# Four graph layers on one core: the order of loads, norms and row preparation where one layer hands over to the next

## The chip, the cores and the metric

The kernel runs on one core of a Trainium2 chip. The metric is the device time of one execution in microseconds (us); lower is better. The core has a matrix engine (TensorE, PE in the profile), a vector engine (DVE), an activation engine (ACT), GpSimd (POOL) and SyncE (SP). Transfers are issued here by SP and by POOL, each into a queue of its own, and run on the same 16 DMA engines. Every engine works through its own instructions in order; an instruction whose input is not ready holds everything behind it on that engine.

## The reference, cut to what matters

A graph with 3327 nodes and 512 features a node passes through four layers. After each one the layer's input is added and every row is normalised.

```python
# layer 0: 8 heads of 64                       layer 2: 8 heads, elu;  layer 3: 4 heads of 128, elu
Wh = einsum('ni,hio->hno', x, W)               # projection
e  = leaky_relu(f1[:, :, None] + f2[:, None, :], 0.2)
att = softmax(where(adj > 0, e, -9e15))        # over the neighbours of a row
y  = einsum('hnm,hmo->hno', att, Wh)
x  = layernorm(x + y)                          # layers 2 and 3: layernorm(x + elu(y))

# layer 1: mean over the first 64 neighbours of a row
keep = (adj > 0) & (cumsum(adj > 0, axis=1) <= 64)
cnt  = keep.sum(axis=1)
xj = leaky_relu((keep @ x / max(cnt, 1)) @ W_nb.T + b_nb)
xi = leaky_relu(x @ W_line.T + b_line)
x  = layernorm(x + xi + where(cnt > 0, xj, 0))
```

## The kernel before, in words

The 3327 rows are padded to 26 tiles of 128 rows, t = 0 to 25; `NT` is 26 and `HALF` is 13. The layers follow one another on the matrix engine. The order of the matrix engine's instructions is written out by hand (`tc.manual_schedule`). The order on the other engines, transfers included, is made by a scheduler from the order in the source and its own estimates of cost; a single instruction can be held in its place in the source with `tc.keep_in_program_order(ins)`, called "pinned" below. Transfers of each issuing engine take eight completion counters in turn, so that a transfer waits at issue until the one eight places before it in the same queue has landed.

**What ends an attention layer.** The attention of layers 0 and 2 leaves sums for 26 tiles in memory (`hd`). The last section's output is copied out of PSUM (`ob`), transposed on the matrix engine (`pt`, L883), copied to `hb` (ACT, L890) and stored to `hd` by SP (L894). The next layer then reads rows back in pairs of tiles, `t0` = 0, 2, 4 and so on. `finish_steps` gives the steps for one pair: load `h` from `hd` and the layer's input as `xr`; divide by the softmax sum (`divide`, DVE, L186); in layers with elu take `e = exp(h)` (ACT, L193); add (DVE, L201 and L202 with elu, L204 without); then `norm_rows`. `norm_rows` takes the statistics of both tiles (DVE, L157 and L158), then one inverse root for the two tiles together (POOL, L148 and L149), the bias (DVE, L162), and scales each tile (ACT, L165).

**Layer 1, `sage`.** First part, per tile: the normed rows are transposed (PE, L1193, `pt`), copied to `xT` (ACT, L1195) and multiplied with the neighbour weights `wn` (PE, L1201, `pz`) and the line weights `wl` (PE, L1204, `pi`); the rows of the next pair are finished alongside. `wn`, `wl` (1 MB each) and the bias `blb` come through POOL's queue. So do the carries `cy` (L1131, 256 KB each), which start the running count of neighbours in a block of columns, and of which the first is used when tile 14 is reached (`carry_in(0)`). SP's queue brings the first mask block `mb` in 13 loads of 64 KB (L1148) and `cr`, one row of counts (L1215, 6.5 KB), which ACT turns to float as `cf` (L1225) for a transpose that stands at t0 = 8. The second part is the neighbour sum (L1303) with the rest of the layer.

**Layer 3, `third`.** For each tile: transposes (PE, L271), copy to `xT` (ACT, L272), a row sum (DVE, L273), and eight matmuls in two banks for the projection (PE, L281, `pw`), then small copies (ACT, L282 and L285) and scaled values (`vt`; DVE L291, ACT L289), which SP stores. The matrix engine is one tile ahead: it transposes tile t and then multiplies tile t - 1. `load_group(t0)` starts the steps of a later pair; its steps run in the source behind the transposes of the pair two earlier. `third` holds `load_group` and calls `finish_steps(..., pinned=t0 == 2)`.

When tile 14 (`HALF + 1`) has been transposed, the columns of the first half are complete, and `L3.prepare(pp, 0)` prepares the row factors: a clamp on DVE and an exponential on ACT over `rc` (`clamp`, L323 and L326), 13 small transposes on PE in quads of four (`quad`, L332, `pr`), a copy of each quad (ACT, L334, `rr`) and its store by SP, then the scales (`scales`, L338 to L346). Behind it stand the load of the first rows `rba` (`rows`, POOL) and `cut` (L369 on), all of them used where the attention of layer 3 begins (L416 and L478).

Of the kernel before, what the change touches and what calls it, by code (L numbers as in the profile page):

```python
# [32 lines left out]
def kernel(  # L33
# [114 lines left out]
        return [nc.gpsimd.tensor_scalar(out, var, LN_EPS, None, op0=ALU.add),  # L148
                nc.gpsimd.tensor_tensor(out, out, power[:, :n], op=ALU.pow)]  # L149

    def norm_rows(pool, ys, t0):
        n = len(ys)
        st = pool.tile([P, 4, 6], F32, name="st")
        mv = pool.tile([P, 4, 2], F32, name="mv")
        rs = pool.tile([P, 4, 2], F32, name="rs")
        for s, y in enumerate(ys):
            nc.vector.bn_stats(out=st[:, s, :], in_=y)  # L157
            nc.vector.bn_aggr(out=mv[:, s, :], in_=st[:, s, :])  # L158
        rsqrt(rs[:, :n, 0], mv[:, :n, 1])
        if t0 + n == NT:  # L160
            nc.vector.tensor_tensor(rs[:, n - 1, 0:1], rs[:, n - 1, 0:1], valid, op=ALU.mult)
        nc.vector.scalar_tensor_tensor(rs[:, :n, 1], mv[:, :n, 0], -1.0, rs[:, :n, 0],  # L162
                                       op0=ALU.mult, op1=ALU.mult)
        for s, y in enumerate(ys):
            nc.scalar.activation(y, y, AF.Identity, bias=rs[:, s, 1:2], scale=rs[:, s, 0:1])  # L165
# [3 lines left out]
    def finish_steps(pool, xin, layer, t0, n, hbufs=6, eng=nc.sync, xbufs=None, xpool=None, ebufs=None, pinned=False,  # L169
                     together=False):  # L170
        H, D = layer.H, layer.D
        ys, xs, steps = [], [], []

        def load():
            for t in range(t0, t0 + n):
                xr = xpool.tile([P, F], F32, name="xr", tag="hb") if xpool else \
                    pool.tile([P, F], F32, name="xr", bufs=xbufs)
                h = pool.tile([P, F], F32, name="h", bufs=hbufs)
                load_tile(h, hd, t, eng)
                ys.append(h)  # L180
                load_tile(xr, xin, t, nc.sync if layer.li == 2 else nc.gpsimd)
                xs.append(xr)

        def divide(s):
            h = ys[s]
            ins = nc.vector.tensor_tensor(h.rearrange("p (h d) -> p h d", h=H), h.rearrange("p (h d) -> p h d", h=H),  # L186
                                          rec[:, t0 + s, :H].rearrange("p (h e) -> p h e", e=1).to_broadcast([P, H, D]),
                                          op=ALU.mult)
            if pinned and t0 > 2:
                tc.keep_in_program_order(ins)  # L190
            if layer.elu:
                e = pool.tile([P, F], F32, name="e", bufs=ebufs)
                ins = nc.scalar.activation(e, h, AF.Exp)  # L193
                if pinned and layer.li == 2 and (t0, s) == (2, 0):
                    tc.keep_in_program_order(ins)
                xs.append(e)

        def add(s):
            h, xr = ys[s], xs[s]
            if layer.elu:  # L200
                nc.vector.scalar_tensor_tensor(xr, xs[n + s], 1.0, xr, op0=ALU.min, op1=ALU.add)  # L201
                nc.vector.scalar_tensor_tensor(h, h, 0.0, xr, op0=ALU.max, op1=ALU.add)  # L202
            else:
                nc.vector.tensor_tensor(h, h, xr, op=ALU.add)  # L204

        steps.append(load)
        if pinned or together:
            steps += [lambda s=s: divide(s) for s in range(n)] + [lambda s=s: add(s) for s in range(n)]
        else:
            for s in range(n):  # L210
                steps += [lambda s=s: divide(s), lambda s=s: add(s)]
        steps.append(lambda: norm_rows(pool, ys, t0))
        return ys, steps

    def finish(*a):
# [897 lines left out]
    def sage(first, first_pool, xin, prev, nxt, wsrc, dst, ring):  # L1113
# [5 lines left out]
        with tc.tile_pool(name="sg_z", bufs=1, reuse_waits="tile") as zp, \  # L1119
# [12 lines left out]
                                    .rearrange("(o t) i -> o t i", o=1).to_broadcast([P, n, GW]))  # L1132
                carry[b, t] = cy

            load_carry()
            load_carry()
            zs_ = [zp.tile([P, HALF, 2, F], F32R, name=f"zs{i}") for i in range(2)]

            def zs(t, c):
# [41 lines left out]
            with tc.tile_pool(name="sa_w", bufs=1, reuse_waits="tile") as wp, \  # L1181
# [37 lines left out]
                for t0 in range(0, NT, 2):  # L1219
                    ys = ahead  # L1220
                    if t0 in (6, 10):
                        prev.late.pop(0)(fp)
                    if t0 == 8:
                        cf = fp.tile([NT, P], F32, name="cf", bufs=1)
                        nc.scalar.copy(cf, cr)  # L1225
                        pt = ps.tile([P, FC, P], F32, name="pt")
                        cb = pt[:, 0, :NT]
                        nc.tensor.transpose(cb, cf, ident[:NT, :NT])
                        nc.vector.tensor_scalar(cnt[:, 0, :], cb, NEIGHBOURS, 1.0, op0=ALU.min, op1=ALU.max)
                        nc.vector.reciprocal(cnt[:, 1, :], cnt[:, 0, :])  # L1230
                        nc.vector.tensor_scalar(cnt[:, 2, :], cb, 0.0, None, op0=ALU.is_gt)
                    for s, y in enumerate(ys):
                        xT = step1(y)
                        if s == 0 and t0 + 2 < NT:
                            ahead = finish(fp, xin, prev, t0 + 2, 2, 6, nc.sync if t0 else nc.gpsimd, None, None, None,
                                           t0 < 6)
                        if pend:
                            step2(*pend)
                        pend = (y, xT, t0 + s)
                        if t0 == NT - 2 * FIRST // 2 - 4 and s == 1:  # L1240
                            seed(qp, "q")
                            carry_in(0)
                            carry_in(1)
                        if t0 + s >= NT - FIRST - 2 and len(kts) < 2 * FIRST:
                            kept()
                            k = len(kts) // 2
                            if k + 1 < FIRST:
                                carry_in(k + 1)
                    if t0 == 0:

                        step2(*pend)
                        pend = None
# [86 lines left out]
    def third(first):  # L1339
        with tc.tile_pool(name="col3", bufs=1) as cp:  # L1340
# [5 lines left out]
            with tc.tile_pool(name="p_w", bufs=1, reuse_waits="tile") as wp, \  # L1346
                    tc.tile_pool(name="p", bufs=3, reuse_waits="tile") as pp, \
                    tc.tile_pool(name="p_f", bufs=2, reuse_waits="tile") as fp, \
                    tc.tile_pool(name="p_ps", bufs=2, space=PSUM, reuse_waits="tile") as ps:
                wsb = wp.tile([P, FC, 2, FW + L3.H], F32, name="wsb")  # L1350

                def bank(e):
                    return ps.tile([P, 512], F32, name=f"pw{e}")


                pend = None
                ahead = first
                groups = []

                def load_group(t0):  # L1360
                    if t0 < NT:
                        groups.append(finish_steps(fp, x2, L2, t0, 2, 10, nc.gpsimd if t0 < 4 else nc.sync, 6,
                                                    pinned=t0 == 2))
                        groups[-1][1].pop(0)()

                load_group(2)
                load_wide(wsb, w3, nc.gpsimd)
                nc.vector.tensor_copy(wsb[:, :, :, FW:], wa[3].rearrange("p c (e h) -> p c e h", e=2))
                load_group(4)
                for t0 in range(0, NT, 2):  # L1370
                    ys = ahead
                    if t0 in (4, 8):
                        L2.late.pop(0)(fp)
                    load_group(t0 + 6)
                    for s, y in enumerate(ys):
                        t = t0 + s
                        store_tile(x3, y, t, nc.sync)
                        xT = L3.project1(pp, ps, y, t)
                        if s == 0 and groups:
                            ahead, steps = groups.pop(0)  # L1380
                            for f in steps:
                                f()
                        if pend:
                            L3.project2(pp, bank, wsb, *pend)
                        pend = (xT, t)
                        if t == HALF + 1:
                            L3.prepare(pp, 0)
                            L3.first_rows = L3.rows(rp, 0, 0)
                            L3.cut(pp, 0, "pc", 1, False, True)
                    if t0 == 0:  # L1390

                        L3.project2(pp, bank, wsb, *pend)
                        pend = None
                L3.project2(pp, bank, wsb, *pend)
                L3.mean(pp, bank, wsb)
# [332 lines left out]
```

## Time and profile before

| | us |
|---|---|
| median of three runs (lowest, highest) | 3219.51 (3215.29, 3220.92) |
| the profiled execution's own time | 3223.41 |
| its span in the trace | 3221.7 |
| PE busy | 3135.2 (97% of the span) |
| DVE, ACT, POOL busy | 2609.5, 2185.6, 322.5 |
| layer 1 begins (first `pz`) | 962.75 after the span's start |
| layer 3 begins (first `pw`) | 2417.45 after the span's start |

All durations in this document come from the profiled execution, whose mean granted clock of the matrix engine was 0.988; its time is 1.7 us more than its span. Line numbers with an L are those of the kernel before.

How the views are read. A **timeline** line gives the start, the busy time, the engine, the line, the operation, and in brackets the idle time of the engine just ahead of the line with what ended it. A line of **waits** says which engine and line waited for which other one, with the total, the number of times and the longest. The **DMA view** of a stretch gives packets and bytes for each queue: q0 is POOL's, q1 is SP's. **Windows** give the busy time of each engine in a stretch and, as PEclk, the share of the matrix engine's clock that was granted.

### The profile page before, as it was taken

To read this page: it belongs to the slowest core of one execution; us is meant where nothing else is said; L and a number is where in the kernel's file an instruction comes from. 1 tells how busy PE (TensorE), PEld (TensorE's weight loads), DVE (VectorE), ACT (ScalarE), POOL (GpSimd) and SP (SyncE) were. 2 spreads that over 40 slices of the span, in tenths; PEclk is the share of its full clock that TensorE was granted. 3 is DMA by queue.
4 is the path that set the end of the run, shared out by engine and by line. 5 is a ranking of instruction groups with operands and counts; after the bars stand their busy time and mean duration, and the time that the engine had idled before them with its cause. 6 is when DMAs were issued, how large, how long until landed. Compare 5 with 4: busy or idle time off the path is not lost. (4 is left out here: it accounts for less than half of the span.)

```text
span 3221.7 us, 44965 instructions
## 1 busy us (share of the span) xinstructions
PE 3135.2 (97%) x17910; PEld 1596.6 (50%) x17910; DVE 2609.5 (81%) x2228; ACT 2185.6 (68%) x1759; POOL 322.5 (10%) x512
## 2 busy tenths in 40 slices
PE   8899999999999999999999999999999999999997
PEld 7643343333334457777744333333337655555543
DVE  5799999999986555555489999999998666678887
ACT  1388889899882222232288889899896655568886
POOL 3110000000011112222220000000002000011211
PEclk9999999999999999999999999999999999999999
DMA  9752113211025345556341110111027311122312
GB/s 363 270 153 75 42 51 123 73 45 43 24 75 153 98 115 146 131 134 160 98 145 61 42 36 20 41 42 42 25 71 247 126 41 43 43 56 93 90 44 69
DMA packets 359985, 301.80 MB, mean 94 GB/s; under 512 B 232756, under 2 KB 291966, under 8 KB 358239
## 3 DMA queue, kind: packets, MB, share of 16 engines
q1 hardware_dynamic: 329471, 194.55, 20.7%
q0 software_dynamic: 24784, 96.68, 9.6%
q10 hardware_dynamic: 5520, 7.69, 0.7%
q8 instruction: 142, 2.33, 0.3%
q14 instruction: 68, 0.56, 0.1%
HBM read 221.97 MB, written 76.84 MB: 93 GB/s over the span
## 5 line engine op out<-in xcount | busy, mean ns | idle before, releaser
L842 ACT ACTIVATE y<-t,bi,sc 128x3328 fp8e4<-128x3328 f32 (+1 forms) x520 | 1336.2, 2604 | 99.4 <-PE pd L819 47.3
L863 PE MATMUL po<-t,vj 128*64 128x448 f32 (+1 forms) x6656 | 1277.4, 523 | 14.0 <-DVE t L841 13.9
L863 PEld LDWEIGHTS po<-t,vj 128*64 128x64 f32 x6656 | 459.3, 137 | 691.7 <-issue 622.7
L478 PE MATMUL po<-t,vj 128*128 128x448 f32 (+1 forms) x1456 | 522.6, 516 | 0.6 <-DVE t L416 0.6
L416 DVE SCALAR_TENSOR_TENSOR t<-rba,qc,mk 128x1664 f32<-128x1664 f32 (+2 forms) x234 | 408.4, 1752 | 125.8 <-PE po L478 88.5
L421 ACT ACTIVATE y<-t,bi,sc 128x1664 fp8e4<-128x1664 f32 (+2 forms) x234 | 375.3, 1618 | 190.1 <-DVE t L416 181.7
L478 PEld LDWEIGHTS po<-t,vj 128*128 128x128 f32 x1456 | 272.1, 190 | 235.2 <-issue 148.8
L841 DVE SCALAR_TENSOR_TENSOR t<-rbb,qc,mask 128x3328 f32<-128x3328 f32 (+1 forms) x130 | 379.9, 2982 | 10.0 <-PE po L863 6.5
L841 DVE SCALAR_TENSOR_TENSOR t<-rbb,qc,mk 128x3328 f32<-128x3328 f32 (+1 forms) x130 | 379.4, 2993 | 8.6 <-PE po L863 6.5
L841 DVE SCALAR_TENSOR_TENSOR t<-rba,qc,mk 128x3328 f32<-128x3328 f32 (+1 forms) x130 | 379.7, 2985 | 5.8 <-PE po L863 3.5
L841 DVE SCALAR_TENSOR_TENSOR t<-rba,qc,mask 128x3328 f32<-128x3328 f32 (+1 forms) x130 | 380.9, 2983 | 4.0 <-PE po L863 3.2
L1303 PE MATMUL acc<-zs,kt 128*128 128x512 f32 x1352 | 360.2, 420 | 0.0
L281 PE MATMUL pw<-wsb,xT 128*128 128x264 f32 (+1 forms) x1248 | 297.7, 393 | 11.8 <-DVE vt L291 8.1
L1161 ACT CAST pk<-cy 128x512 f32<-128x512 bf16 x169 | 99.6, 590 | 288.4 <-DVE kt L1175 281.9
L1303 PEld LDWEIGHTS acc<-zs,kt 128*128 128x128 f32 x1352 | 255.6, 189 | 52.1 <-PE pk L1154 0.8
L819 PE MATMUL pd<-y,sden 128*32 128x384 fp8e4 (+1 forms) x3328 | 270.2, 343 | 0.0
L281 PEld LDWEIGHTS pw<-wsb,xT 128*128 128x128 f32 x1248 | 238.4, 194 | 54.8 <-issue 6.5
L1175 DVE SCALAR_TENSOR_TENSOR kt<-pk,mb 128x512 fp32r<-128x512 f32 x169 | 115.9, 686 | 107.1 <-PE pk L1172 107.0
L819 PEld LDWEIGHTS <-sden 128*32 128x32 bf16 x3328 | 89.0, 95 | 166.7 <-issue 151.2
L291 DVE TENSOR_TENSOR vt<-pw,dc 128x256 f32<-128x256 f32 x130 | 49.8, 417 | 78.1 <-ACT dc L282 76.0
L1201 PE MATMUL pz<-wn,xT 128*128 128x512 f32 x208 | 94.0, 595 | 7.7 <-ACT xT L1195 3.7
L1131 POOL DMA_DIRECT2D cy<-ctd x91 | 70.1, 770 | 267.3 <-ACT pk L1161 243.4
(244 smaller groups left out, 2163.6 us busy)
## 6 DMA issues: line engine op xcount, KB each, us to landing
raw<-in_adjT_dram SPq DMA_DIRECT2D x67, 416.0 KB
vj<-v SPq DMA_DIRECT2D x169, 128.0 KB
cy<-ctd POOLq DMA_DIRECT2D x78, 256.0 KB, 4.3
h<-hd SPq DMA_DIRECT2D x61, 256.0 KB
v<-vt SPq DMA_DIRECT2D x50, 256.0 KB
md<-mask SPq DMA_DIRECT2D x26, 416.0 KB
mb<-md SPq DMA_DIRECT2D x169, 64.0 KB
mk<-md SPq DMA_DIRECT2D x50, 208.0 KB
```

Of the source, the lines that this page charges most:

```text
L281: nc.tensor.matmul(pw[e][:, :FW + H], xT[:, c, :], wsb[:, c, e, :], start=c == 0, stop=c == FC - 1)
L416: ins = nc.vector.scalar_tensor_tensor(t[:, :w], rb[:, lo:lo + w], self.qc[:, j, h:h + 1], mask_at[0](j, i0 + lo, w), op0=ALU.max, op1=ALU ...
L421: nc.scalar.activation(y[:, :w], t[:, :w], AF.Sigmoid, bias=self.bi[:, j, h:h + 1], scale=self.sc[:, j, h:h + 1], saturate=False)
L478: nc.tensor.matmul(po[c][k * D:(k + 1) * D, :z - a_], vj[:, j % 2, k * D:(k + 1) * D], ts[k][:, a_:z], start=j == 0, stop=j == NT - 1)
L819: nc.tensor.matmul(pd[c][32 * kk:32 * kk + 32, :w_], lhsT, rhs, start=(kk, c) not in seen, stop=last and j == NT - 1)
L841: nc.vector.scalar_tensor_tensor(to, ro, self.qc[:, j, h:h + 1], m, op0=ALU.max, op1=ALU.mult)
L842: nc.scalar.activation(yo, to, AF.Sigmoid, bias=self.bi[:, j, h:h + 1], scale=self.sc[:, j, h:h + 1], saturate=False)
L863: nc.tensor.matmul(po[c][k * D:(k + 1) * D, :z - a_], vj[:, j % 2, x_:x_ + D], t[:, k, a_:z], start=j == 0, stop=j == NT - 1)
L1161: nc.scalar.copy(pks[k % 2], carry[b, t // 4 * 4][:, t % 4:t % 4 + 2, :])
L1175: nc.vector.scalar_tensor_tensor(kt, pk, NEIGHBOURS, mb[:, t:t + 2, :], op0=ALU.is_le, op1=ALU.mult)
L1201: nc.tensor.matmul(pz, xT[:, c, :], wn[:, c, :], start=c == 0, stop=c == FC - 1)
L1303: nc.tensor.matmul(acc, kts[b, t][:, s * P:(s + 1) * P], zs(t, c), start=t == 0 and c == 0, stop=t == NT - 1 and c == 1)
```

## The change

Four things are done. The first two carries are loaded at t0 = 6 of `sage` instead of ahead of `wn` and `wl`. The first pair of tiles (t0 = 0) of layers 0 and 2 is normed one tile at a time, with an inverse root for each tile, and in layer 2 its statistics are pinned. In `divide`, the pin that was asked for with `pinned and t0 > 2` is asked for with `pinned or layer.li == 2 and t0 == 4`; `load_group` passes `pinned` for t0 = 2, so the divides of the pairs t0 = 2 and t0 = 4 of layer 2 are now held in the order of the source. In `third`, the clamp of `prepare` stays behind tile 14 and the rest of `prepare`, the load of the first rows and `cut` stand behind tile 15.

```diff
-    def norm_rows(pool, ys, t0):
+    def norm_rows(pool, ys, t0, pinned=False):
...
-            nc.vector.bn_aggr(out=mv[:, s, :], in_=st[:, s, :])
+            ins = nc.vector.bn_aggr(out=mv[:, s, :], in_=st[:, s, :])
+            if pinned:
+                tc.keep_in_program_order(ins)
...
-            if pinned and t0 > 2:
+            if pinned or layer.li == 2 and t0 == 4:
                 tc.keep_in_program_order(ins)
...
                 steps += [lambda s=s: divide(s), lambda s=s: add(s)]
-        steps.append(lambda: norm_rows(pool, ys, t0))
+                if t0 == 0 and layer.li != 3:
+                    steps.append(lambda s=s: norm_rows(pool, ys[s:s + 1], t0 + s, layer.li == 2))
+        if t0 or layer.li == 3:
+            steps.append(lambda: norm_rows(pool, ys, t0))
...
-            load_carry()
-            load_carry()
...
+                    if t0 == 6:
+                        load_carry()
+                        load_carry()
                     for s, y in enumerate(ys):
                         xT = step1(y)
...
                         if t == HALF + 1:
-                            L3.prepare(pp, 0)
+                            parts = L3.prepare_steps(pp, 0)
+                            parts.pop(0)()
+                        if t == HALF + 2:
+                            for f in parts:
+                                f()
                             L3.first_rows = L3.rows(rp, 0, 0)
                             L3.cut(pp, 0, "pc", 1, False, True)
```

On the matrix engine the order differs in one place only: the 13 transposes of L332 stand one tile later. What the built program does with the order on the other engines is told in the prediction.

## Prediction

> **What bounds the kernel now.** I read the page's first part, the waits around both passages, and there the timelines of each engine, the DMA view and the clock.
>
> ```profile
> PE 3135.2 (97%) x17910; PEld 1596.6 (50%) x17910; DVE 2609.5 (81%) x2228; ACT 2185.6 (68%) x1759; POOL 322.5 (10%) x512
> ```
>
> The matrix engine is busy for 97% of the span, so the change is worth what it takes from or adds to PE's few idle stretches. In the waits of 950 to 980 us, where layer 1 begins, these stand:
>
> ```profile
> PE pz L1201 <- ACT xT L1195: 2.9, 1, 2.9
> ...
> PE pz L1201 <- DMA wn<-in_wnT_dram: 2.7, 1, 2.7
> ACT cf L1225 <- DMA cr<-ctd: 2.6, 1, 2.6
> PE pt L883 <- ACT hb L890: 2.5, 1, 2.5
> ```
>
> PE loses 2.53 + 2.67 + 2.90 = 8.1 us here. The third line is ACT waiting for the row of counts; it harms nobody, as ACT makes `cf` after both `xT`. SP's timeline and the DMA view of 962 to 969 us show why that row is late:
>
> ```profile
> 958.98 7.59 SPq L894 DMA_DIRECT2D hd<-hb  x3
> 966.63 4.84 SPq L1148 DMA_DIRECT2D mb<-md  x6
> 971.79 0.33 SPq L1215 DMA_DIRECT2D cr<-ctd  x1
> ```
>
> ```profile
> q0 software_dynamic: 694, 2.43, 86.6%
> q1 hardware_dynamic: 675, 0.38, 17.5%
> ```
>
> While POOL's large loads drain, both queues advance about 97 packets/us (694/7 and 675/7), but POOL's packets are 4 KB and SP's 512 bytes or so. SP's first `hd` store (512 packets) takes 957.15 to 968.22. The layer 3 passage, on PE's timeline:
>
> ```profile
> 2410.53 0.33 PE L883 MATMUL pt<-ident,ob 128*128 128x128 f32 x1 [1.27 <-ACT hb L890]
> 2415.65 1.97 PE L271 MATMUL pt<-ident,h 128*128 128x128 f32 x8 [4.79 <-ACT h L165]
> 2417.45 9.35 PE L281 MATMUL pw<-wsb,xT 128*128 128x260 f32 x32
> ...
> 2433.56 0.66 PE L271 MATMUL pt<-ident,h 128*128 128x128 f32 x4 [1.13 <-ACT h L165]
> ```
>
> and its windows, where the column behind the five engines is the granted clock:
>
> ```profile
> 2409.00:2415.60 6.60, 0.60 (x4) 0.17 (x2) 4.54 (x11) 1.67 (x4) 0.96 (x2) 0.68 0.95 291
> 2415.60:2420.00 4.40, 4.35 (x14) 3.64 (x15) 4.37 (x9) 3.83 (x7) 0.00 (x0) 0.50 0.93 333
> 2420.00:2424.00 4.00, 4.00 (x15) 3.29 (x15) 3.41 (x8) 1.11 (x6) 2.73 (x2) 0.79 0.93 305
> ```
>
> The two first projections take 9.35 us where later ones take 3.67 each (2434.05): 2.0 us are lost to the clock after the wait. The row preparation costs two waits:
>
> ```profile
> 2481.89 1.04 PE L332 MATMUL pr<-ident,rc 128*4 128x128 f32 x8 [1.98 <-ACT rc L326]
> 2483.47 1.22 PE L332 MATMUL pr<-ident,rc 128*4 128x128 f32 x5 [0.55 <-ACT rr L334]
> ```
>
> **A. Layer 1's start.** The built order has `wn` where the first carry stood, so it is issued at about 953.3 instead of 955.64. The norm by tiles frees `hb` from both L165 (1.52 us): the 2.53 us wait goes. It adds a POOL pair (0.23 + 0.73) and a DVE L162 (0.16), beside idle stretches of both. The carries (two issues of 0.80) come on POOL after the next pair's loads, and stay due only at tile 14, past 1050 us; free.
>
> Two orders change besides. ACT now has `cf` ahead of both `xT`, and SP has five `mb`, three `hd`, eight `mb`, then `cr`. The last three `mb` wait for the three `hd` to land, and `cr` follows them. So a new wait stands on ACT, with `xT`(0), hence `pz`(0), behind it. Its price: `hd`(0) is issued at about 954.7 (`hb` no longer 2.5 us late). The three stores are 512 + 512 + 128 = 1152 packets. Before, the first packet moved 4.7 us after issue; so 959.4. POOL holds 832 packets of 4 KB (`wn`, `wl` 256 each, `blb`, two `h`, two `xr` 64 each); at the 184 of the first five us and 95/us then, it is done at about 966, at 95/us throughout by 964. Until then SP passes 460 to 660, the rest at 730/us (970 to 971). The last store lands a us later (as `hd`(0) did): 966 to 968. `cr` is issued half a us on, and lands 2.0 (an undisturbed `mb`, 948.14 to 950.05) to 3.5 us (its own before) later: 968.5 to 972, I take 971. `cf` 0.30 and `xT` 0.58 put `pz`(0) at 971.9; `pz`+`pi` take 7.1, `pz`(1) is at 979.0 instead of 972.75: +6.2. `wn` lands at 958 to 961 (256 packets at the same two rates), but nothing can use it before `xT`(0): the 2.53 and 2.67 taken away are swallowed by this wait. All later tiles follow without slack (gaps of 0.29 and 0.44). After some 13 us of idle PE I add the 2.0 of clock, from nothing (`pz`(1) after 2.90 us took 3.70, no loss) to 2.0. **+8.2**, from +3.7 to +12.4 (`cr` at its old 975.25).
>
> The page "TensorE: Matmul & The Clock Gate" of the Trainium skill (Part 1) says that about 3.4 us of idle halve the clock and about 3.4 us of work restore it. That agrees with the 0.50 above; by it the loss is an estimate of 1.7 us, and A would be +7.9. The page "DMA: Bandwidth & Descriptors" (Queues, rings and completion order) says that an engine alternates between queues packet by packet. The 694 and 675 agree, and it speaks against this order: early 4 KB packets delay SP's small ones whoever needs them.
>
> **B. First pair of layer 3.** L157(0), L158(0) now stand ahead of the second tile's. From L158 to L165 takes 1.65 us (2413.13 to 2414.78). With L157 at 2407.98 and L158 at 2409.2, L165(0) ends at 2411.6. The second `hb` is queued behind it, so the `hb` wait grows from 1.27 to about 2.4. Tile 1's L158 is at 2412.0, its L165 ends at 2414.4, and its transposes end at 2415.1, where `pw` starts: **-2.3**, from -4.3 (clock regained too) to 0.
>
> **C. The pinned divides.** Before, the divide of pair 4 ran at 2416.05, when its rows had come. Now it stands on DVE behind the row sum of tile 2 and the divides of pairs 6 and 8. `pw` 0 and 1 end at 2424.5, tile 2's transposes at 2425.1, its `xT` at 2425.7, the sum (0.67) at 2426.4. Then, at DVE's 0.6 an instruction: the first divide ends at 2427.0; L273, a divide of pair 8, L201, L202 and the second divide end at 2430.0; L157, L291 (0.4), L201 and L158 (0.2) at 2431.8; L201, L202, L202, L157 and L201, partly for pair 6, at 2434.7, where L158 of the second tile stands. Plus 1.65 and 0.76, tile 4 is normed at 2437.1. PE, free at 2429.5, waits 7.6 us there; tile 4's transposes move from 2433.56 to 2437.1: +3.5 with B in it. Clock +2.0, later waits absorbed (0.93, 0.28, 0.38 up to 2450) -1.6: B and C together **+4.0**, from -3.3 (C hidden: -2.3 and a us of absorbed waits) to +8.
>
> **D. Preparation in two parts.** Clamp and exponential run a tile (4 us) earlier than PE asks: -1.98. The third quad waits for the first copy L334, which ACT has behind the last tile's small copies, two `vt` (1.1) and now two `e` (0.6 each): about 1.5 to 2 us instead of 0.55. The 13 transposes (2.3), four copies (0.3 to 0.5), their SP stores, POOL's row load and the casts move 4 us towards first use at 2536, some 45 us away: covered. **-0.5**, from -2.6 (both waits and 0.6 of clock; `pw` 4.25 against 3.67) to +3 (the two `e` and a pair of L165, 2.7 us of ACT's work, all fall between quad and copy).
>
> Sum: 8.2 + 4.0 - 0.5 = **+11.7**. The profiled execution would go from 3223.4 to 3235.1; it lies 3.9 above the median of the three runs, 3219.5, which goes to **3231**.
>
> **The rivals.**
> *Faster.* `cr` is quick: the last store is issued at 956.6, lands in 2.0, `cr` half a us later in 2.0: 961.1, `pz`(0) at 962.0, no wait ahead of `pz`(1), A is -3.6. With B -2.3, a us absorbed, C hidden and D -1, the sum is -8: 3211.5. For it: `hd` stores start earlier. Against it: they travel while POOL drains. The deciding point: `cr` landed by 964.7.
> *Only A.* Pair 4 is normed in time: 8.2 - 3.3 - 0.5 = +4.4, 3224. For it: DVE idles there (1.18 at 2425.9). Against it: the built order.
> *A and C cancel.* `cr` quick, pair 4 late: -3.6 + 4.0 - 0.5, about 0: 3219.5.
> *Dearer.* `cr` lands no earlier than before (A +12.4) and D costs 3: +19, 3239.
>
> **How the numbers follow.** Chances: forecast 0.55 (its own range 3225 to 3237), faster 0.13, only A 0.18, cancel 0.07, dearer 0.07. A measurement here can tell about 0.2%, 6.4 us. Over that: forecast 0.52, only A 0.08, dearer 0.07, so slower 0.67. Within: forecast 0.02, only A 0.10, cancel 0.05: 0.17. Faster: 0.01 + 0.13 + 0.02 = 0.16. The range 3213 to 3240 leaves out half of the faster case and half of the dearer one.
>
> **What would show it.** PE's first `pz` waiting for ACT's `xT`, and ACT's `cf` for `cr`, until about 971; a PE wait of 7 to 8 us ahead of tile 4's L271 with clock near 0.5 behind it; no wait for `rc` at L332, but one for `rr`. The forecast is wrong if `cr` lands before 965 or pair 4's L165 runs before 2430.

## The result, and the profile after

| | kernel before | changed kernel |
|---|---|---|
| median (lowest, highest), six executions each | 3220.28 (3215.29, 3225.95) | 3243.69 (3241.81, 3248.76) |
| the profiled execution, and its span | 3223.41, 3221.7 | 3241.81, 3240.1 |
| first L883 of layer 0's end to the second `pz` | 19.20 | 30.37 |
| first L883 of layer 2's end to the first L478 | 129.08 | 136.66 |
| everything else in the span | 3073.4 | 3073.1 |

The changed kernel is slower: 1.0071 times the kernel before, 95% interval 1.0061 to 1.0081. Measured again beside other runs it gave 1.0068 (1.0056 to 1.0081). In the two traces the difference is 18.4 us, all of it in the two passages (11.2 and 7.6; the rest is 0.3 less). That the rest agrees so well is partly luck: over all fourteen traces of this document it lies between 3070.4 and 3079.3. The medians differ by 23.4 because the profiled execution of before lies 3.1 above its median and that of the changed kernel 1.9 below its own.

From here on, lines of the changed kernel carry its own numbers: L1193 to L1225 are now L1196 to L1228, L165 is L167, L186 L188, L271 L276, L281 L286, L332 L337, L334 L339, L478 L483, L883 L888 (kernels with further edits can be a few lines off). The text keeps the names L478 and L883 for these two places in every kernel. PE's timeline where layer 1 begins:

```profile
956.59 0.60 PE L1196 MATMUL pt<-ident,h 128*128 128x128 f32 x4
957.96 0.66 PE L1196 MATMUL pt<-ident,h 128*128 128x128 f32 x4 [0.76 <-ACT h L167]
975.91 5.80 PE L1204 MATMUL pz<-wn,xT 128*128 128x512 f32 x8 [17.30 <-ACT xT L1198]
```

The 2.53 us wait for `hb` is gone, and in its place PE stands for 17.30 us, waiting for ACT's `xT`. ACT's and SP's timelines say why:

```profile
975.09 0.30 ACT L1228 CAST cf<-cr 26x128 f32<-26x128 bf16 x1 [15.14 <-DMA cr<-ctd]
975.29 1.05 ACT L1198 COPY xT<-pt 128x512 f32<-128x512 f32 x2
```

```profile
955.91 1.76 SPq L899 DMA_DIRECT2D hd<-hb  x3
957.73 13.12 SPq L1151 DMA_DIRECT2D mb<-md  x8
970.95 0.38 SPq L1218 DMA_DIRECT2D cr<-ctd  x1
```

ACT waited 15.14 us for a row of 6.5 KB. SP spent 13.12 us on eight mask loads, since the last three had to wait until the three `hd` stores had landed (the last one at 970.2); then it issued `cr`, and that took another 4 us. The DMA view of 962 to 968.5 us, and then of 971 to 973:

```profile
q0 software_dynamic: 667, 2.25, 86.7%
q1 hardware_dynamic: 686, 0.34, 17.9%
```

```profile
q0 software_dynamic: 191, 0.63, 98.5%
q1 hardware_dynamic: 47, 0.01, 3.0%
```

The first pair is the alternation of before. What POOL's queue held longer than the forecast had it is on POOL's timeline: the two moved carries are issued right behind the loads of the next pair.

```profile
958.99 0.54 POOL L126 DMA_DIRECT2D xr<-in_x_dram  x1
959.52 0.77 POOL L1136 DMA_DIRECT2D cy<-ctd  x1
960.64 0.75 POOL L1136 DMA_DIRECT2D cy<-ctd  x1 [0.36 <-DMA wn<-in_wnT_dram]
```

The 832 packets of 4 KB that the forecast counted had started by 966.9; the carries' 128 kept the queue going until 968.6. In the second pair POOL's next loads move (an `xr`, a carry and an `xr`, issued at 967.21, 967.75 and 969.25), and for two microseconds SP's queue passed 47 packets. In part that is SP's own: its last mask packets started at 971.3, and what it had issued behind them, `cr` first, only at 972.8, 1.85 us after `cr`'s issue, where the first packet of an undisturbed mask load started 1.0 us after its own (949.16 for 948.14). That POOL's loads make the rest is not shown by a run of its own.

In layer 3's passage, on PE's timeline:

```profile
2422.80 0.33 PE L888 MATMUL pt<-ident,ob 128*128 128x128 f32 x1 [2.59 <-ACT hb L895]
2423.25 0.63 PE L276 MATMUL pt<-ident,h 128*128 128x128 f32 x4
2425.11 1.11 PE L276 MATMUL pt<-ident,h 128*128 128x128 f32 x4 [1.23 <-ACT h L167]
2426.01 9.56 PE L286 MATMUL pw<-wsb,xT 128*128 128x260 f32 x32
```

```profile
2449.59 1.11 PE L276 MATMUL pt<-ident,h 128*128 128x128 f32 x4 [7.51 <-ACT h L167]
2450.49 5.77 PE L286 MATMUL pw<-wsb,xT 128*128 128x260 f32 x16
...
2456.53 3.67 PE L286 MATMUL pw<-wsb,xT 128*128 128x260 f32 x16
```

```profile
2499.93 1.04 PE L337 MATMUL pr<-ident,rc 128*4 128x128 f32 x8
2506.18 1.22 PE L337 MATMUL pr<-ident,rc 128*4 128x128 f32 x5 [5.21 <-ACT rr L339]
```

The first `pw` comes 7.79 us after layer 2's first L883 (2418.22), where it was 10.17 (2407.28 to 2417.45). Then PE waits 7.51 us for tile 4 and pays 2.1 more on the next projection (5.77 against 3.67). At the row preparation the wait for the exponential is gone, and the one for the copy has grown from 0.55 to 5.21.

### The profile page after: what moved, and what is told of

Same layout as the page of the kernel before. It is cut to its first block, busy times and chain, and to the rows that moved or that the text cites. A ratio compares the mean times of both kernels' runs of the same rounds, so it can differ in the third digit from the quotient of the medians.

```text
span 3240.1 us, 44988 instructions
## 1 busy us (share of the span) xinstructions
PE 3136.6 (97%) x17910; PEld 1600.5 (49%) x17910; DVE 2611.9 (81%) x2230; ACT 2188.5 (68%) x1759; POOL 318.2 (10%) x516
## 3 DMA queue, kind: packets, MB, share of 16 engines
q8 instruction: 142, 2.33, 0.3%
## 5 line engine op out<-in xcount | busy, mean ns | idle before, releaser
L483 PE MATMUL po<-t,vj 128*128 128x448 f32 (+1 forms) x1456 | 522.6, 516 | 0.6 <-DVE t L421 0.6
L483 PEld LDWEIGHTS po<-t,vj 128*128 128x128 f32 x1456 | 272.1, 190 | 235.2 <-issue 148.5
L286 PE MATMUL pw<-wsb,xT 128*128 128x264 f32 (+1 forms) x1248 | 299.2, 395 | 13.2 <-DVE vt L296 9.9
L286 PEld LDWEIGHTS pw<-wsb,xT 128*128 128x128 f32 x1248 | 239.8, 196 | 55.7 <-issue 7.4
```

The costliest lines, as they stand in the source:

```text
L286: nc.tensor.matmul(pw[e][:, :FW + H], xT[:, c, :], wsb[:, c, e, :], start=c == 0, stop=c == FC - 1)
L483: nc.tensor.matmul(po[c][k * D:(k + 1) * D, :z - a_], vj[:, j % 2, k * D:(k + 1) * D], ts[k][:, a_:z], start=j == 0, stop=j == NT - 1)
```

## The experiments

Each was run beside the kernel before; a ratio is to that kernel, with its 95% interval. "Second `pz`" is counted from the first L883 of layer 0's end, and "L478" from the first L883 of layer 2's end.

**1. The cast held at its place.** SP's and POOL's orders at layer 1's start are those of the changed kernel.

```diff
-                        nc.scalar.copy(cf, cr)
+                        tc.keep_in_program_order(nc.scalar.copy(cf, cr))
```

> The changed kernel with one line more: the cast of the row of counts (cf) is held at its place in the source, t0 = 8, so it no longer stands ahead of both xT copies; SP's and POOL's queues are unchanged. Theory (the wait for cr on ACT makes layer 1 late): the 17.3 us wait ahead of the first pz is replaced by about 2 us for wn (pz at about 961) and by about 3 us ahead of the second pz, whose xT waits for the last hd store; the second pz starts near 971 instead of 985, about -14 us, to a median near 3230. Rival (the early 1 MB loads starve everything in SP's queue, and the cast is only the first to show it): the second pz stays at 980 or later, the median above 3239.

Measured: 1.0018 (1.0008 to 1.0027), median 3227.73. PE's timeline of this kernel:

```profile
959.80 6.60 PE L1204 MATMUL pz<-wn,xT 128*128 128x512 f32 x8 [1.97 <-DMA wn<-in_wnT_dram]
966.24 3.60 PE L1207 MATMUL pi<-wl,xT 128*128 128x512 f32 x8
970.11 3.70 PE L1204 MATMUL pz<-wn,xT 128*128 128x512 f32 x8 [0.27 <-ACT xT L1198]
```

The second `pz` is at 16.30. The theory holds, and the rival falls: with the transfers in the same order, the place of one instruction on ACT makes 14 us. The wait that was expected ahead of the second `pz` was nearly hidden by a slow first one (6.60 for 3.67).

**2. Pair 4's divides free.**

```diff
-            if pinned or layer.li == 2 and t0 == 4:
+            if pinned:
```

> The changed kernel with the pin taken from the divides of pair 4 only (pair 2's stay pinned). Theory (DVE order makes tile 4 late): its divides go back ahead of the first row sum, the 7.5 us wait ahead of tile 4's transposes falls to at most 1.5, the projection behind it runs at 3.7 us instead of 5.8; about -7.5 us, to a median near 3236. Rival (pair 4's rows land late because SP's queue is reordered): the wait stays at 5 us or more, the median above 3241.

Measured: 1.0045 (1.0030 to 1.0060), median 3234.70, 9.0 under the changed kernel.

```profile
2426.42 1.12 PE L276 MATMUL pt<-ident,h 128*128 128x128 f32 x4 [3.98 <-ACT h L167]
2427.32 8.39 PE L286 MATMUL pw<-wsb,xT 128*128 128x260 f32 x32
...
2443.90 0.66 PE L276 MATMUL pt<-ident,h 128*128 128x128 f32 x4 [1.14 <-ACT h L167]
2444.39 1.92 PE L286 MATMUL pw<-wsb,xT 128*128 128x260 f32 x8
```

Tile 4 now waits 1.14 us, as in the kernel before (1.13), so the theory holds; L478 is at 131.50. The wait ahead of the third quad has changed too, from 5.21 to 3.50 (see run 3). But the free divide goes ahead of tile 1's statistics and waits there for its rows, so tile 1 comes 2.75 us later (3.98 against 1.23) and the early start of layer 3 is lost. The pin buys one and costs the other.

**3. The preparation in one piece.**

```diff
-                            parts = L3.prepare_steps(pp, 0)
-                            parts.pop(0)()
-                        if t == HALF + 2:
-                            for f in parts:
-                                f()
+                            L3.prepare(pp, 0)
```

> The changed kernel with the preparation of the row factors behind tile 14 in one piece, as before. Theory (the later place puts more of ACT's work between the quads and their copies): the 5.2 us wait ahead of the third quad falls to under 1, about 2 us of wait for the exponential return; -2.5 us, to a median near 3241. Rival (the pins shift ACT's order all the way down, and the split is innocent): a wait of 4 us or more stays, the median within 1 us of the changed kernel's 3243.7.

Measured: 1.0059 (1.0044 to 1.0074), median 3239.78. The wait for the exponential does not return, and the third quad still waits 3.47 us for the copy.

```profile
2495.28 1.04 PE L337 MATMUL pr<-ident,rc 128*4 128x128 f32 x8
2499.80 0.75 PE L337 MATMUL pr<-ident,rc 128*4 128x128 f32 x5 [3.47 <-ACT rr L339]
```

L478 is at 136.31, 0.35 earlier than in the changed kernel, but a second trace of that same kernel (run 9) has it at 139.29, so such a difference says nothing. Neither side had it right: the other edits to layer 3 shift ACT's order here, to 3.47 us of wait instead of 2.53 for both waits of before, and the split adds 1.7 on top. That 1.7 is not the split's alone: with the split and pair 4's divides free (run 2) the wait is 3.50, with the split alone (run 8) 3.49, and only the split with the pin of pair 4 makes 5.21.

**4. The first two together.**

> The edits of the first two together. Theory (two separate causes): -14 and -7.5 add up, to a median near 3222, within 0.2% of the kernel before. Rival (one delay hides part of the other): less than -17 in all, above 3227.

Measured: 1.0005 (0.9993 to 1.0016), median 3222.86. The two causes add up within what can be told: one by one they measured -16.0 and -9.0, together they make -20.8, and the intervals do not settle the 4 us between.

**5. Layer 1's edits alone, with the cast at its place.** Beside the edit of the first run, the edits to layers 2 and 3 are undone.

> Only the two edits that touch layer 1's start (carries at t0 = 6, layer 0's first pair normed one tile at a time) with the cast of the row of counts held at its place; layers 2 and 3 are as in the kernel before. Theory (the edits do what their words say once the cast is out of the way): the second pz starts 16.4 us after the first L883 instead of 19.2, layer 3's passage costs what it cost before; -3 to -6 us, ratio 0.998 to 0.999. Rival (the time is given back in the neighbour sum, whose counts and masks come later): within 1 us of the kernel before.

Measured: 0.9996 (0.9987 to 1.0005), median 3220.74. The second `pz` is at 16.58 and L478 at 128.51, as the theory has it; but the rest of the span is 3073.5, as before, and the gain in time is not distinguishable from none.

**6. Layer 1's edits alone, the cast free.**

> The same two edits without holding the cast. Theory: the first pz waits about 17 us for xT behind the cast, the second pz starts 30 us after the first L883 instead of 19.2; +10 us, ratio 1.003, and with the layer 3 edits' part of about 8 to 10 this makes up the changed kernel. Rival (the passages disturb each other): +5 or less, or +15 or more.

Measured: 1.0029 (1.0017 to 1.0040), median 3231.62; second `pz` at 31.05, L478 at 128.04. The theory holds.

**7. The carries alone.** The kernel before, with its two first `load_carry()` moved to t0 = 6.

> The kernel before with the two carries at t0 = 6 and nothing else. In the built order the cast stays behind both xT. Theory (it takes both edits together to bring the cast ahead): no wait for cr; wn lands 2 us earlier, the second pz starts up to 3 us earlier; -1 to -3 us. Rival (the early 1 MB loads alone starve SP's stores): the second pz is later than before, +3 or more.

Measured: 1.0006 (0.9997 to 1.0015), median 3223.82. The second `pz` is at 15.96, 3.2 us earlier. But ACT's cast waits for `cr` here too, one step further on, now ahead of the norm of tiles 2 and 3:

```profile
974.06 0.30 ACT L1223 CAST cf<-cr 26x128 f32<-26x128 bf16 x1 [5.50 <-DMA cr<-ctd]
974.26 1.51 ACT L165 ACTIVATE h<-h,rs 128x512 f32<-128x512 f32 x2
975.69 1.04 ACT L1203 CAST zs<-pz 128x512 fp32r<-128x512 f32 x2
```

```profile
976.28 0.69 DVE L1204 TENSOR_TENSOR zs<-pz,zs 128x512 fp32r<-128x512 f32 x1 [5.48 <-ACT zs L1203]
```

```profile
988.39 1.11 PE L1191 MATMUL pt<-ident,h 128*128 128x128 f32 x4 [4.00 <-ACT h L165]
```

The casts of `zs` behind it hold DVE, which finishes the next pair late, and PE waits 4.00 us at tile 4 (0.44 in the kernel before). The carries alone do not bring the cast ahead of `xT`, but the same wait eats the gain a little later. Whether the norm by tiles alone would bring it ahead was not run, so that it takes both edits is not shown.

**8. The split alone.** The kernel before with the preparation in two parts.

> The kernel before with the preparation in two parts and nothing else. Theory (ACT has more ahead of the first quad's copy at the later place, whatever the pins do): no wait for the exponential at the first quad, but about 3.5 us ahead of the third quad; together 3.5 against 2.5 before, +1 us, within what can be measured. Rival (the split pays when the pins are absent): waits of 1 us or less, -2 us.

Measured: 1.0002 (0.9993 to 1.0011), median 3223.66. The first quad does not wait, the third waits 3.49; L478 is at 130.15, 1.1 later.

```profile
2486.45 1.03 PE L332 MATMUL pr<-ident,rc 128*4 128x128 f32 x5 [3.49 <-ACT rr L334]
```

The theory holds for the waits; the time cannot be told from the kernel before.

**9. The changed kernel again.**

> The changed kernel itself, beside the same runs of the kernel before as the next three. Theory (the two passages' losses add): layer 1's edits alone measured 1.0029, the layer 3 edits 1.0018 over 0.9996 with layer 1 mended, so the sum is 1.005, a median of 3238 to 3240. Rival (the first measurement stands, and one passage makes the other dearer): 1.007 again, near 3244.

Measured: 1.0068 (1.0056 to 1.0081), median 3242.77. In this trace the second `pz` is at 30.32 and L478 at 139.29. The number is the rival's. But the sum of the theory was made with too small a value for layer 3; with the one of run 11 it is 0.29% + 0.34% = 0.63%, inside the interval, and in the traces each passage costs alone what it costs here (31.05 in run 6, 137.18 in run 11). The passages add.

**10. The row of counts first.** Its load is written ahead of the mask blocks; in the built order it is the fourth of them, ahead of the `hd` stores.

```diff
+            cr = zp.tile([NT, P], BF, name="cr")
+            nc.sync.dma_start(out=cr, in_=ctd[NT:NT + 1, :].rearrange("o (t p) -> (o t) p", p=P))
             for t in range(0, NT, 2):
                 load_block(0, t)
```

> The changed kernel with the load of the row of counts issued among the first mask blocks, ahead of the hd stores; the cast still stands ahead of both xT. Theory (it is the late arrival that costs, the place alone costs the cast's 0.3 us): no wait for cr, the second pz 16.4 us after the first L883 as in the first experiment, -16 us against the changed kernel. Rival (the cast's place or the queue behind it costs by itself): the second pz more than 25 us after.

Measured: 1.0029 (1.0019 to 1.0039), median 3230.95; against 3242.77 beside it, -11.8 where -16 was expected; the intervals of the two leave room for that.

```profile
956.55 0.29 ACT L1228 CAST cf<-cr 26x128 f32<-26x128 bf16 x1
...
959.44 0.59 ACT L1200 COPY xT<-pt 128x512 f32<-128x512 f32 x1
970.25 0.58 ACT L1200 COPY xT<-pt 128x512 f32<-128x512 f32 x1 [10.21 <-DMA mb<-md]
```

The cast is still early and costs its 0.29: it is the arrival that costs, not the place. The second `pz` is at 16.68. The second `xT` now waits 10.21 us. The view names a mask load, but the semaphores that this `xT` waits for include those of two `hd` stores, of which the later landed at 970.07: its memory is most likely that of a `hb`, which has to be stored first. This is the 2.90 us wait of the kernel before, and it is still there (3.33).

**11. Layer 3's edits alone.**

> The edits at layer 3's start alone (first pair of layer 2 normed one tile at a time, pinned divides of pairs 2 and 4, preparation in two parts); layer 1's start as before. Theory: first pw 2.4 us earlier after layer 2's end, 7.5 us of wait ahead of tile 4, 5.2 us ahead of the third quad, and about 4 us of clock; +7 us, ratio 1.0022. Rival (the passages disturb each other in the changed kernel, alone they cost less): +3 or less.

Measured: 1.0034 (1.0021 to 1.0047), median 3231.22; L478 at 137.18, waits of 7.52 ahead of tile 4 and 5.21 ahead of the third quad. The rival falls, and the theory was too low by some 3 us.

**12. All of it mended.** The cast held; the divides of pairs 2 and 4 pinned, those of pair 4 issued behind tile 1's row sum; the preparation in three parts.

```diff
-            if pinned or layer.li == 2 and t0 == 4:
+            if pinned:
...
-                                                    pinned=t0 == 2))
+                                                    pinned=t0 in (2, 4)))
...
+                        if t == 1:
+                            for _ in range(2):
+                                groups[0][1].pop(0)()
...
                         if t == HALF + 2:
+                            parts.pop(0)()
+                            parts.pop(0)()
+                        if t == HALF + 3:
                             for f in parts:
                                 f()
```

> All edits of the change with three repairs: the cast held at its place, the divides of pairs 2 and 4 both pinned but those of pair 4 issued behind tile 1's row sum, and the preparation in three parts (clamp behind tile 14, two quads behind 15, the rest behind 16). Theory: second pz 16.4 us after the first L883 (-2.8), first pw 2.4 us earlier, no wait over 1.5 us ahead of tile 4, none at the quads (-2.5): -6 to -8 us in all, ratio about 0.998. Rival (waits freed at these places come back as waits for the next engine, as in the fifth run): within 0.1% of the kernel before.

Measured: 0.9999 (0.9990 to 1.0008), median 3222.24. Every named wait fell as the theory has it: second `pz` at 16.72, first `pw` at 7.79, 1.39 ahead of tile 4, none at the quads. And yet L478 is at 129.17, where it was 129.08. PE's waits in that passage (2406 to 2536 us):

```profile
PE pt L276 <- ACT h L167: 5.2, 4, 1.6
PE pw L286 <- ACT xT L277: 3.8, 4, 1.7
PE pt L888 <- ACT hb L895: 2.8, 2, 2.6
PE pw L286 <- DVE vt L296: 1.4, 2, 1.0
```

They sum to 13.2 us; the kernel before has 12.3 there in the same view. The rival holds: taken away at one place, the waits come back at `xT` and `vt`. No version here beats the kernel before by more than a measurement can tell; runs 4, 5, 7, 8 and 12 cannot be told from it.

## Why the prediction was right or wrong

The direction and the three mechanisms were right, and each stands on runs of its own: the cast (1 and 10), the pinned divides (2), the quad's copy (3 and 8). The size was wrong: +11.7 was forecast for the profiled execution, the traces show +18.4 and the medians +23.4, beyond the range's end of 3240. Three steps failed: the landing of `cr`, for which the carries were put at nothing; the place of tile 4's wait; and the work on ACT ahead of the quad's copy. Term by term, from the two traces (a second trace of the same kernel has L478 2.6 us later, so B to D are good to a few us only):

**A, forecast +8.2 (3.7 to 12.4), measured +11.2.** What was said to be swallowed was swallowed. The term that was mis-sized is the landing of `cr`, 971 in the forecast and about 975 in the trace (974 on the clock of before, whose first L883 is 1.06 earlier). The prediction called the carries free, as they are due only at tile 14, and left them out of POOL's queue, though it had them issued right behind the loads that it counted. The 832 packets drained as forecast (966.9, which is 965.9 on the clock of before, for 964 to 966); with the carries it took until 968.6. That put the last `hd` store some 1.2 us later (an estimate: when the 832 had started, 597 of the stores' 1152 packets had too, and behind the drain the last 342 took 0.8 us). The rest is mainly `cr`'s own way, 4 us from issue to landing for a forecast 2.0 to 3.5. The clock loss of A, 2.0 in the forecast, was 2.1 (5.80 against 3.67; in the four other traces with this wait 2.0 to 2.9). Alone, over the whole kernel, these edits cost 9.4 in the medians (run 6).

**B, forecast -2.3, measured -2.4** (7.79 against 10.17), with the longer wait for `hb` (2.59 for a forecast 2.4).

**C, forecast +4.0 with B.** The wait ahead of tile 4 is 7.51 for a forecast 7.6, its clock loss 2.1 for 2.0. What failed is where the wait stands: tile 4's transposes were to start 3.5 later than before, counted from layer 2's end, and start 5.1 later (31.37 against 26.28). The count took tiles 2 and 3 as ready when PE came to them. But pair 2's pinned divides stand behind tile 0's row sum, PE waits 0.96 for tile 2 as well (0.53 before) and 0.40 for an `xT`, and two projections took 9.56 instead of 9.35. On DVE's timeline the divide of tile 4 is at 2438.88 and that of tile 5 at 2442.00, 3.1 us apart where 3.0 was reckoned:

```profile
2438.88 0.68 DVE L188 TENSOR_TENSOR h<-h,rec 128x512 f32<-128x512 f32 x1
...
2442.00 0.68 DVE L188 TENSOR_TENSOR h<-h,rec 128x512 f32<-128x512 f32 x1
```

B and C together are +5.2 at the last projection ahead of the preparation (16.17 later there against 10.94 at layer 2's end).

**D, forecast -0.5 (-2.6 to +3), measured +2.4.** The wait for the exponential went as forecast; the one ahead of the third quad is 5.21 and not 1.5 to 2. ACT's timeline shows what stands between the last tile's `xT` and the copy:

```profile
2501.93 0.42 ACT L385 CAST pc<-rest 128x52 bf16<-128x52 f32 x1 [1.45 <-DVE rest L384]
2502.07 1.52 ACT L167 ACTIVATE h<-h,rs 128x512 f32<-128x512 f32 x2
2503.49 0.61 ACT L195 ACTIVATE e<-h 128x512 f32<-128x512 f32 x1
2504.32 0.63 ACT L195 ACTIVATE e<-h 128x512 f32<-128x512 f32 x1 [0.21 <-DVE h L188]
```

The two exponentials had been counted. The two norms had been put at the range's end only, and the cast of `cut`, which waits 1.45 us for DVE, had been called covered; both belonged in the sum. Runs 2 and 3 add that 1.7 us of this wait need the pin of pair 4 beside the split, so D is not independent of C.

A, B with C, and D make 18.8, less 1.3 that came back between the passages, plus 1.06 from ahead of layer 0's end: the 18.6 by which the last matmuls are later. The remaining 5 us to the difference of the medians lie in where the two profiled executions stand among their fellows; the range had no room for that.

The rivals: "faster" and "cancel" fell with the first wait. "Only A" is refuted by run 11. "Dearer", with 0.07, came nearest: it has `cr` landing at its old 975 (it landed at 974 on that clock) and D at +3 (+2.4).

## What to carry to other kernels

When a scheduler orders the queues, read the built order of every engine for an instruction that moved ahead of the critical one, and price it by the landing of what it waits for: a cast of 0.3 us whose result is needed 55 us later (at 1030.14) held PE for 17. Small transfers behind large ones of another queue should be priced at packets, and with every load in that queue or still to come into it, also those whose own result is due late: the two carries were such loads. Measure edits alone and together: the carries alone gave 1.0006, with the norm by tiles 1.0029, as there the cast came ahead of `xT`.

## What the runs showed of the hardware

The same wait does not always cost clock. The first `pz` took 3.67 us after a wait of 2.67 in the kernel before, and 5.37 after 2.85 in run 8, whose layer 1 passage is the same code; runs 1 and 10 gave 6.60 and 3.67 after waits of 1.97 and 2.00. Of the nine traces with a wait of 1.7 to 3.4 us at this place, two lost nothing, five lost 1.7 us, and two 2.8 and 2.9.

The traces' record of the granted clock shows what differs. It is 1.00 or 0.50 in all fourteen, and as long as PE works, the half clock comes in stretches of 3.41 us or a whole multiple, up to 20.48. Within one trace the starts of these stretches lie whole multiples of 3.41 us apart from the first to the last, whatever was done between; against the kernel this grid lies differently in each trace. In the kernel before, the half clock is over when the first `pz` begins (962.75):

```profile
957.34:960.75 3.41, 2.75 (x13) 2.34 (x12) 1.15 (x3) 1.60 (x4) 3.20 (x6) 0.50 0.79 196
960.75:964.16 3.41, 1.41 (x4) 0.72 (x5) 0.00 (x0) 0.00 (x0) 0.00 (x0) 1.00 1.04 411
```

In run 8 a second stretch falls on it (963.56):

```profile
957.52:960.93 3.41, 3.03 (x13) 2.63 (x13) 1.46 (x3) 1.93 (x5) 3.41 (x7) 0.50 0.84 149
960.93:964.35 3.42, 0.79 (x2) 0.49 (x3) 0.00 (x0) 0.00 (x0) 0.10 (x1) 1.00 1.03 410
964.35:967.76 3.41, 3.41 (x5) 1.35 (x4) 0.00 (x0) 0.00 (x0) 0.00 (x0) 0.50 1.04 400
```

Past the first L478, where no kernel here differs in order from another on PE, nine of the fourteen traces need 684.7 to 685.7 us and five 687.3 to 687.8, so one step of 2 us there. It stands at one place, 603 to 610 us past L478, behind a wait for DVE of 2.33 us in all fourteen and a second one of up to 1.36: the mean granted clock of that stretch is 1.00 in six traces, 0.76 in three and 0.55 to 0.59 in the five that need longer, and up to the last matmul it is 1.00 everywhere else past L478. The same waits with the same instructions cost 2 us in one execution and nothing in another. So two executions of one kernel can differ by about what the edits of layer 1 save with the cast held (2.6 us in run 5's trace).

The Trainium skill ("TensorE: Matmul & The Clock Gate", Part 1) has the clock follow a free-running window of about 3.4 us. The stretches of 3.41 us on one grid agree. The 1.7 that one such window at half clock would lose (an estimate from that page) is what five traces lost at the first `pz`; in run 1 two windows on end, 958.87 to 965.70, lie on it. The prediction took from the page that about 3.4 us of idle halve the clock; here waits from 1.7 us on came with half clock, and so did the windows that follow those with PE busy for 0.88 us of 3.41 (before, 953.93 to 957.34) and for 1.59 (run 1, 955.46 to 958.87). As one with 1.41 (before, above) was not, the busy time alone does not decide it, and what does stays open.
